# Sums of four rows through TensorE instead of VectorE, thirteen tile places instead of fourteen, and another order

## The chip, the core and the metric

The kernel runs on one core of a Trainium2 chip. Its engines are TensorE (PE, with its weight loads as PEld), VectorE (DVE), ScalarE (ACT), GpSimd (POOL) and SyncE (SP, which here only issues transfers). The metric is the device time of one execution in microseconds (us), the median of several runs; lower is better.

## The reference

The input x is [8, 512, 1024] in float32. Each of the 8 batches is cut into 8 blocks of 64 tokens, and the blocks are summed. The 64 sums go through one matrix (Wk), are normalised, scored against a query vector and turned by a softmax into 8 weights for each batch. The weighted sum of the blocks goes through a second matrix (Wo) and gives one row p of 1024 numbers for each batch, which is added to every token of the batch. Then comes a layer norm, and x itself is added:

```python
block_repr = inputs.reshape(B, n_blocks, block_size, H).sum(axis=2)
keys = jnp.einsum('bnh,kh->bnk', block_repr, Wk)
rms = jnp.sqrt(jnp.mean(keys * keys, axis=-1, keepdims=True) + EPS)
scores = jnp.einsum('bnh,h->bn', keys / rms * rms_weight, q)
attn = jax.nn.softmax(scores, axis=-1)
attended = jnp.einsum('bn,bnh->bh', attn, block_repr)
proj = jnp.einsum('bsh,kh->bsk', broadcast(attended), Wo)
x = inputs + proj
out = (x - mean(x)) / jnp.sqrt(var(x) + EPS) * ln_gamma + ln_beta
return inputs + out
```

## The kernel before, in words

The 4096 tokens are 32 rows of 128 tokens, each a [128, 1024] piece of float32, numbered 0 to 31. Two rows form a tile of 1 MB, and tiles live in places of SBUF (`XSLOTS`, line 20: fourteen). The eight tiles of the two weight matrices (w0 for Wk, w1 for Wo) pass through the same places ahead of the rows. The batches are taken in three groups of 2, 4 and 2 (`GROUPS`, line 19): rows 0 to 7, 8 to 23, 24 to 31; x1.3 is tile 3 of group 1. Rows are finished in units of four or two (`UNITS`, line 21): unit 0 has rows 0 to 3, unit 2 rows 8 to 11, unit 3 rows 12 to 15, unit 7 rows 28 and 29, unit 8 rows 30 and 31.

Each group n goes through these steps, whose names the texts use (n or the row's number k stands behind the letter):

- bs: PE sums a tile's tokens into the block sums in PSUM (line 429); col turns them into columns (DVE, line 439).
- proj n.0: the blocks times Wk (PE, line 473). The softmax steps sm n follow: sq, qk, sdd, mm, v, ln, ex, n1, n2, n3, sc, mx, ex0, rc, wc, small steps that pass between ACT, DVE, POOL and PE (lines 492 to 518). proj n.1: the blocks times Wo; v n w scales the result by the weights (line 529). For group 0 the weights must first be transposed: T0.e and T1.e are the eight transposes by PE of one piece of a matrix, with a copy from PSUM by ACT or DVE.
- p n mm: PE spreads p to all 128 partitions in PSUM (line 545), two copies (cp0, cp1) bring it to SBUF as `pb`, and four small transfers (tb) put its rows into a table `tab` beside gamma and beta.
- S k: DVE adds p to row k in place and sums the result (line 646). Q k: ACT squares the sum less its mean and sums the squares (line 648).
- Unit steps U q: variance (v), its root (std) and inverse root (rs) by POOL, the statistics table (s2, sd2), its transposes by PE (mm, line 721) and their copy to SBUF (lt). Unit 8 takes logarithm and exponential on ACT (ln, ex) instead.
- D k: DVE writes (gamma + std) times row k into a pair of PSUM banks (line 746). R k: PE adds the terms with mean, beta and p, two rows at once (line 732). E k: ACT scales the result by rs back into the row's place (line 761). A store of each finished tile follows on SP.

There are three pairs of PSUM banks and two single ones; a step that needs a pair waits until the last user has read it. Fillers are matmuls of zeros (line 869) between the real ones on PE.

Every step is put down once with the engines that can do it, and the order in which all engines get their steps is written out as one string of step numbers (`ORDER`, line 43; a letter picks the engine, a number behind a colon the bank, f, h and z are fillers). Each engine works through its steps in that order and waits where an operand or a place is not free. Loads are issued by SP in the order of `LOADS` (line 35).

The code already has a kind 'p' of unit (line 633) beside the kind 'c' that all nine units use (`UKIND`, line 26). In kind 'p' the row is not rewritten: its sum is taken from x alone ahead of time (B k), and x + p exists only in PSUM:

```python
for h in range(2):
    nc.tensor.matmul(pair(y)[:, h, :].rearrange("p (q d) -> p q d", d=P), ident, bands(x_row(k))[:, :, h, :],
                     start=True, stop=False, skip_group_check=True)
spread_p(G, y, False)
```

Of the kernel before, what the change touches and what calls it, by code (L numbers as in the profile page):

```python
# [903 lines left out]
```

## Time and profile before

| | us |
|---|---|
| median of 3 runs | 146.02 (145.58 to 146.04) |
| the profiled execution | 144.9 |
| its span | 143.2 |
| PE, DVE, ACT, POOL busy | 112.3, 95.5, 90.9, 58.5 |

The page gives the busy time of each engine over the whole span. Windows give the same for a stretch, the timeline gives single instructions with what ended the idle time before them, and the list of groups gives the mean of one instruction of a form. The mean granted clock of TensorE was 0.932 of full speed.

### The profile page before, as it was taken

What the parts mean: (1) busy time and instruction counts of PE and PEld (TensorE: products, weight loads), DVE (VectorE), ACT (ScalarE), POOL (GpSimd) and SP (SyncE); (2) the same over time, 40 slices, a digit from 0 to 9 for tenths busy, and PEclk for the clock granted to TensorE, in tenths of its full rate; (3) what the DMA queues carried; (4) which work ended last, traced back from release to release, by engine and by line L of the source; (5) the groups of instructions that cost most, each with busy time, mean ns of one, the idle gap of its engine ahead of it and who ended that gap; (6) DMA issues with size and microseconds to landing.
All of it is one profiled execution on the core that took longest, in us unless ns stands there. A gap on an engine that the chain in (4) does not pass through costs nothing.

```text
span 143.2 us, 2871 instructions
## 1 busy us (share of the span) xinstructions
PE 112.3 (78%) x1093; PEld 58.9 (41%) x1101; DVE 95.5 (67%) x161; ACT 90.9 (64%) x140; POOL 58.5 (41%) x107
## 2 busy tenths in 40 slices
PE   7869853989999685999693989989798498496820
PEld 2539652947985222544340335443252132122300
DVE  3040312311315996928879999999999999997930
ACT  3022520024931898255689989899989989989630
POOL 6888800000000066652000895566506928809100
PEclk9995999599999999999999599999999869999965
DMA  4999999999999999605499870724770850775993
...
DMA packets 7526, 42.76 MB, mean 299 GB/s; under 512 B 808, under 2 KB 808, under 8 KB 3672
## 3 DMA queue, kind: packets, MB, share of 16 engines
...
## 4 chain that ended last, share of the span: by engine, by line
DMA 33%; PE 24%; DVE 17%; ACT 11%; issue 6%; POOL 3%; SPq 2%; DVEq 0%; ACTq 0%
PE b L473 11%; DVE t L746 9%; DMA gam<-in_L_cond_ln_gamma_dram 8%; DMA x<-in_L_cond_Wo_dram 8%; DMA x<-in_L_cond_Wk_dram 6%; DMA x<-in_x_dram 5%; PE t L732 5%; PE t L407 4%; ACT x L761 4%; DVE x L646 4%; ACT square L648 3%; DMA tab<-in_L_cond_ln_gamma_dram 3%; DMA pb<-in_cond_dram 3%; ACT woT L241 2%; PE b L429 1%
## 5 line engine op out<-in xcount | busy, mean ns | idle before, releaser
L746 DVE SCALAR_TENSOR_TENSOR t<-gam,ustd,x 128x1024 f32<-128x1024 f32 x31 | 39.1, 1291 | 3.7 <-ACT x L761 2.5
L648 ACT ACTIVATE square<-x,tot 128x1024 bf16<-128x1024 f32 x32 | 36.7, 1147 | 3.3 <-DVE x L646 2.1
L646 DVE SCALAR_TENSOR_TENSOR x<-x,pb 128x1024 f32<-128x1024 f32 x32 | 37.6, 1223 | 0.1
L761 ACT ACTIVATE x<-t,urs 128x1024 f32<-128x1024 f32 x31 | 33.2, 1107 | 5.5 <-PE t L732 2.4
L700 POOL TENSOR_SCALAR stat<-tot 128x8 f32<-128x8 f32 (+1 forms) x8 | 7.5, 934 | 53.1 <-DVE x L646 53.0
L732 PE MATMUL t<-tab,lt 32*128 32x512 f32 x124 | 24.9, 667 | 4.8 <-DVE lt L243 2.2
L407 PE MATMUL t<-ident,x 128*128 128x128 f32 x120 | 17.9, 316 | 5.3 <-DMA x<-in_L_cond_Wk_dram 3.0
L869 PE MATMUL b<-zeros 128*128 128x512 bf16 (+1 forms) x57 | 18.2, 439 | 2.1 <-DVE zeros L294 1.0
L407 PEld LDWEIGHTS t<-ident,x 128*128 128x128 f32 x120 | 16.9, 202 | 6.6 <-issue 4.7
L869 PEld LDWEIGHTS <-zeros 128*128 128x128 bf16 x87 | 8.7, 108 | 17.2 <-issue 12.8
L695 POOL TENSOR_TENSOR ustd<-uv,halfs 128x4 f32<-128x4 f32 (+1 forms) x8 | 13.3, 1660 | 5.5 <-DVE uv L692 4.1
L732 PEld LDWEIGHTS t<-tab,lt 32*128 32x128 f32 x124 | 7.5, 191 | 16.9 <-DVE t L746 5.7
L241 ACT COPY wkT<-t 128x1024 f32<-128x1024 f32 x5 | 5.1, 1013 | 14.1 <-PE t L407 14.1
L715 POOL TENSOR_TENSOR urs<-uv,halfs 128x4 f32<-128x4 f32 (+1 forms) x8 | 13.2, 1650 | 0.0
L243 DVE COPY wkT<-t 128x1024 f32<-128x1024 f32 x3 | 3.7, 1225 | 12.1 <-PE t L407 12.1
L429 PE MATMUL b<-x,blk 128*32 128x256 f32 x128 | 8.4, 384 | 4.2 <-DMA x<-in_x_dram 3.7
L473 PE MATMUL b<-wkT,blkT 128*32 128x256 f32 x192 | 11.0, 380 | 0.6 <-DVE blkT L439 0.6
L241 ACT COPY woT<-t 128x1024 f32<-128x1024 f32 x6 | 5.8, 1014 | 7.8 <-PE t L407 7.8
L429 PE MATMUL t<-x,blk 128*32 128x256 f32 x128 | 7.9, 382 | 3.1 <-DMA x<-in_x_dram 3.1
L473 PEld LDWEIGHTS b<-wkT,blkT 128*32 128x32 f32 x192 | 5.9, 110 | 5.8 <-issue 1.2
L473 PE MATMUL b<-woT,blkT 128*32 128x256 f32 x128 | 7.9, 382 | 0.0
L869 PE MATMUL t<-zeros 128*128 128x512 bf16 x22 | 6.4, 380 | 1.1 <-ACT lt L241 0.6
...
## 6 DMA issues: line engine op xcount, KB each, us to landing
...
```

Of the source, the lines that this page charges most:

```text
L241: nc.scalar.copy(dst, src)
L407: nc.tensor.transpose(half(part, c // 4)[:, bass.ts(c % 4, P)], tile_of(name)[:, e % RT, c::HC], ident)
L429: nc.tensor.matmul(bank(f"bs{n}")[32 * j : 32 * j + 32, :QU], blk[G["g"]], tile_of(name)[:, r, bass.ts(j, QU)], start=(t == 0 and r == 0), ...
L473: nc.tensor.matmul(bank(name)[32 * j : 32 * j + 32, :QU], b[:, c, :], w[:, c, j], start=(c == 0), stop=(c == HC - 1),)
L646: add(f"S{k}", [(DVE, 1.15)], lambda e: nc.vector.scalar_tensor_tensor(x_row(k), x_row(k), 1.0, pb[n], ALU.mult, ALU.add, accum_out=total) ...
L648: add(f"Q{k}", [(ACT, 1.28)], lambda e: nc.scalar.activation(square, x_row(k), AF.Square, bias=total, scale=-float(H), accum_out=ssq), rea ...
L695: add(f"{T} std", [(POOL, 0.5 + 0.16 * U)], lambda e: nc.gpsimd.tensor_tensor(std, v, halfs[:, :1].to_broadcast([P, U]), ALU.pow), reads=[ ...
L715: add(f"{T} rs", [(POOL, 0.5 + 0.16 * U)], lambda e: nc.gpsimd.tensor_tensor(rs, v, halfs[:, 1:].to_broadcast([P, U]), ALU.pow), reads=[V, ...
L732: nc.tensor.matmul(half(f"row{k}", h), lts[q % NST][lo : lo + 32, r // RT, :], tab_of(k)[0][lo : lo + 32, :], start=False, stop=True, skip ...
L746: add(f"D{k}", [(DVE, 1.21)], lambda e: nc.vector.scalar_tensor_tensor(flat(pair(name)), gam, std, x_row(k), ALU.add, ALU.mult), reads=["g ...
L761: add(f"E{k}", [(ACT, 1.13)], lambda e: nc.scalar.activation(x_row(k), flat(pair(name)), AF.Identity, scale=rs), reads=[RS], writes=[xk(k) ...
L869: nc.tensor.matmul(bank_at(i)[:, :n], zeros, zeros[:, 0:1].to_broadcast([P, n]), start=start, stop=True, skip_group_check=True)
```

## The change

Unit 3 (rows 12 to 15) becomes of kind 'p'. Its four S and the Q's that read SBUF go. In their place come B12 to B15, the sums of x alone, each on ACT or DVE; Bp1.0, the sum of p; U3 to, which adds the two sums on POOL; Y12 to Y15 on PE, two matmuls of the row by the identity and the four matmuls of p into the same pair of banks; Q12 to Q15, which square from PSUM; U3 sn, one more small step on POOL; tx1, which multiplies the table by gamma (DVE, 128x512) for this unit's R; and gx, a table of gamma that it needs (one memset and four small loads). `XSLOTS` goes from 14 to 13, some small tiles share storage (`kw` and `diag` now lie in `vw0`), and other kinds and switches that are not used come in. The core of the diff:

```diff
-XSLOTS = 14
+XSLOTS = 13
-UKIND = 'ccccccccc'
-TABS = ((0, 'y'), (1, 'y'), (2, 'y'))
-FORMS = ('y',)
+UKIND = 'cccpccccc'
+TABS = ((0, 'y'), (1, 'x'), (1, 'y'), (2, 'y'))
+FORMS = ('x', 'y')
...
-    kw = alloc("kw", [P, QU], BF16) if junk is None else junk[:, :QU]
+    kw = vw[0]
...
-        elif kind_of(k) == "p":
-            add(f"B{k}", [(ACT, 1.28)], lambda e: nc.scalar.activation(square, x_row(k), AF.Identity, accum_out=usx[u][:, r : r + 1]),
+        elif kind_of(k) in "pa":
+            sx = usx[u][:, r : r + 1]
+            add(f"B{k}", [(ACT, 1.34), (DVE, 1.2)], lambda e: nc.scalar.activation(
+                square, x_row(k), AF.Identity, accum_out=sx) if e == ACT else nc.vector.tensor_reduce(sx, x_row(k), AX.X, ALU.add),
                 reads=[xk(k)], writes=[f"usx{u}.{r}"])
...
-        if mine & set("bp"):
-            add(f"Bp{n}.0", [(ACT, 1.28)], lambda e: nc.scalar.activation(square, pb[n % 2], AF.Identity, accum_out=t[:, 0:1]),
+        if mine & set("bpa"):
+            add(f"Bp{n}.0", [(ACT, 1.34), (DVE, 1.2)], lambda e: nc.scalar.activation(
+                square, pb[n % NPB], AF.Identity, accum_out=t[:, 0:1]) if e == ACT else nc.vector.tensor_reduce(
+                t[:, 0:1], pb[n % NPB], AX.X, ALU.add),
```

The order string is another one. Told by engines, with the steps around the change (S, D and so on of consecutive rows drawn together):

```
DVE before, from the first softmax to S0: qk sdd v n1 n2 n3 sc mx | T1.7 cp0 | rc wc | v0 w | p0 cp0 | S0
DVE after:   qk sdd | T1.6 cp | v | T1.3 cp | n1 n2 n3 sc mx | T1.7 cp1 cp0 | rc wc | B12 B13 | v0 w | B14 | p0 cp1 | S0
DVE before, from S7: S7 | gamma scaled | col1 | D0-D2 | sm1 qk sdd | D3 | v | D4 | n2 n3 sc mx | D5 | U1 lt | rc wc | D6 D7 | S8-S15 | D8 D9 | col2 | D10 | S16-S18 | D11 D12 | sm2 qk | S19 ...
DVE after:   S7 | col1 | U0 lt | D0-D2 | U1 v | sm1 qk sdd v | D3 | n1 n2 n3 sc mx | D4 | rc wc | D5 D6 | p1 cp1 cp0 | S8-S11 | D7 | S16 | tx1 | S17-S19 | D8 D9 | U2 lt | col2 | D10 | S20 | D11 D12 | U3 lt | sm2 qk | S21 ...
ACT after, from E4: E4 E5 | Bp1.0 | Q8 Q15 Q10 Q14 Q9 Q11 | E6 E7 | Q13 Q19 Q12 Q16 | E8 E9 | Q20 | sm2 sq | Q18 | E10 E11 ...
PE before, from R4: R4 | p1 mm | bs2.0 bs2.1 | R6 | bs2.2 | 9 fillers | bs2.3 | U2 mm | R8 | proj2.0 ...
PE after:    R4 | p1 mm | Y15 Y14 | bs2.0 bs2.1 | R6 | Y13 | bs2.2 | Y12 | U2 mm | bs2.3 | R8 | proj2.0 ...
PE, group 0: before T1.7 | proj0.1 | bs1.0 | p0 mm; after T1.7 | bs1.0 | proj0.1 | bs1.1 | p0 mm
SP before: x2.0 | tb0 | x2.1 | st1 st3 | x2.2 | tb1 with st5 | x2.3 | st7 ...
SP after:  x2.0 | tb0 | st1 st3 | x2.1 | st5 | tb1 | x2.2 x2.3 | st7 ...
```

The scaling of gamma goes from DVE to ACT (behind Q5), both copies of p1 from ACT to DVE, the copies lt of units 2, 3, 4 and 7 from ACT to DVE, U1's from DVE to ACT, U7 v from DVE to POOL. In the tail ACT now does U8 ln, E26, U8 ex where it did U8 ln, U8 ex, E26.

## Rows read from the trace of the kernel before

**Rows 1.** The page: busy time, share of the span, instructions of each engine.
```profile
PE 112.3 (78%) x1093; PEld 58.9 (41%) x1101; DVE 95.5 (67%) x161; ACT 90.9 (64%) x140; POOL 58.5 (41%) x107
```

**Rows 2.** Windows: start:end, length, busy of each engine, clock, DMA share, GB/s.
```profile
73.60:128.80 55.20, 45.31 (x339) 18.29 (x334) 54.64 (x84) 51.58 (x80) 30.30 (x28) 0.94 0.56 230
```

**Rows 3.** Groups by form: busy us, mean ns, idle before and its releaser.
```profile
L746 DVE SCALAR_TENSOR_TENSOR t<-gam,ustd,x 128x1024 f32<-128x1024 f32 x31 | 39.1, 1291 | 3.7 <-ACT x L761 2.5 <-ACT u L484 0.8 <-PE t L869 0.3
L646 DVE SCALAR_TENSOR_TENSOR x<-x,pb 128x1024 f32<-128x1024 f32 x32 | 37.6, 1223 | 0.1
L648 ACT ACTIVATE square<-x,tot 128x1024 bf16<-128x1024 f32 x32 | 36.7, 1147 | 3.3 <-DVE x L646 2.1 <-ACT lt L241 0.5 <-ACT square L648 0.3
L761 ACT ACTIVATE x<-t,urs 128x1024 f32<-128x1024 f32 x31 | 33.2, 1107 | 5.5 <-PE t L732 2.4 <-POOL urs L715 1.3 <-issue 1.1
...
L780 DVE TENSOR_SCALAR x<-b,urs 128x512 f32<-128x512 f32 x2 | 1.4, 749 | 0.6 <-PE b L732 0.6
```

**Rows 4.** Timeline of DVE: start us, length us, engine, line, operation.
```profile
75.92 1.22 DVE L646 SCALAR_TENSOR_TENSOR x<-x,pb 128x1024 f32<-128x1024 f32 x1
...
77.07 1.22 DVE L646 SCALAR_TENSOR_TENSOR x<-x,pb 128x1024 f32<-128x1024 f32 x1
...
82.80 2.49 DVE L746 SCALAR_TENSOR_TENSOR t<-gam,ustd,x 128x1024 f32<-128x1024 f32 x2
...
124.75 0.42 DVE L243 COPY lt<-b 128x256 f32<-128x256 f32 x1
125.09 1.22 DVE L646 SCALAR_TENSOR_TENSOR x<-x,pb 128x1024 f32<-128x1024 f32 x1
```

**Rows 5.** Timeline of ACT: two squares in a stream, two scalings.
```profile
76.17 1.15 ACT L648 ACTIVATE square<-x,tot 128x1024 bf16<-128x1024 f32 x1
...
77.45 1.15 ACT L648 ACTIVATE square<-x,tot 128x1024 bf16<-128x1024 f32 x1
...
79.87 2.10 ACT L761 ACTIVATE x<-t,urs 128x1024 f32<-128x1024 f32 x2
```

**Rows 6.** Timeline from the second matrix's transposes to col1, PE and DVE.
```profile
33.60 2.03 PE L407 MATMUL t<-ident,x 128*128 128x128 f32 x16
...
39.30 3.70 PE L459 MATMUL t<-woT,blkT 128*32 128x192 f32 x128
...
45.74 1.23 DVE L646 SCALAR_TENSOR_TENSOR x<-x,pb 128x1024 f32<-128x1024 f32 x1
...
52.36 1.07 PE L429 MATMUL t<-x,blk 128*32 128x256 f32 x16 [0.66 <-DMA x<-in_x_dram]
...
54.88 1.07 PE L429 MATMUL t<-x,blk 128*32 128x256 f32 x16 [1.13 <-DMA x<-in_x_dram]
...
56.14 0.69 DVE L352 TENSOR_SCALAR gam<-gam 128x1024 f32<-128x1024 f32 x1 [1.10 <-DMA gam<-in_L_cond_ln_gamma_dram]
...
56.75 0.44 DVE L439 STREAM_TRANSPOSE blkT<-t 128x256 f32<-128x256 f32 x1
```

**Rows 7.** Timeline of PE from p1's matmuls to proj2.0.
```profile
71.12 1.13 PE L545 MATMUL b<-vw,spread 64*128 64x256 f32 x8
...
78.43 1.07 PE L429 MATMUL b<-x,blk 128*32 128x256 f32 x16 [2.49 <-DMA x<-in_x_dram]
...
83.31 1.07 PE L429 MATMUL b<-x,blk 128*32 128x256 f32 x16
84.32 0.44 PE L721 MATMUL b<-ident,stat 128*128 128x128 f32 x2
...
86.50 3.66 PE L473 MATMUL b<-wkT,blkT 128*32 128x256 f32 x64
```

**Rows 8.** Windows, one late stretch, columns as in rows 2.
```profile
110.00:116.00 6.00, 4.14 (x17) 1.73 (x17) 6.00 (x9) 5.97 (x9) 4.98 (x4) 0.79 0.74 308
```

**Rows 9.** Timeline of SP's queue: the loads of x2.2 and x2.3.
```profile
70.08 0.38 SPq L272 DMA_DIRECT2D x<-in_x_dram  x1
...
76.14 1.25 SPq L272 DMA_DIRECT2D x<-in_x_dram  x1
```

More of the change, by code (lines that the diff above doesn't have):

```diff
@@ L32 @@
 UP = 32768.0
+ADD_ISSUE = 1.3
+BY_PE = ()
+ROOT_POW = ()
+DIVIDE = False
+ADD_MB = 2.0
 SINGLE = (28, 29, 30)
@@ L388, in table @@
                 out=t[32 * q + 2 : 32 * q + 2 + g, :], in_=p[0:P:w, i * HALF : (i + 1) * HALF]),
-                reads=[f"pb{n % 2}.{j}" for j in range(2)], writes=[f"tab{n % NTAB}.{q}"], mb=0.01)
+                reads=[f"pb{n % NPB}.{j}" for j in range(2)], writes=[f"tab{n % NTAB}.{q}"], mb=0.01)
         if (n, "x") in TABS:
@@ L464, in project @@
                     add(f"{name}.{at}.{c0}.{qs}.{cs}", [(PE, 0.012 * cs + 0.108 * qs * cs)], lambda e, go=go: go(),
-                        reads=[f"blkT{n % 2}"] + w_keys(which, range(2 * at, 2 * (at + qs)), halves[0]),
+                        reads=[f"blkT{n % NBT}"] + w_keys(which, range(2 * at, 2 * (at + qs)), halves[0]),
                         claim=("b", name) if at == c0 == 0 else None, use=[] if at == c0 == 0 else [name])
@@ L477, in project @@
             add(f"{name}.{c0}", [(PE, 0.98)], lambda e, go=go: go(),
-                reads=[f"blkT{n % 2}"] + w_keys(which),
+                reads=[f"blkT{n % NBT}"] + w_keys(which),
                 claim=None if c0 else ("b", name), use=[name] if c0 else [])
@@ L514, in softmax @@
             cs, cs, AF.Exp, bias=mx, scale=-1.0, accum_out=es), reads=["mx"], writes=["cs", "es"])
[L515 removed]
+        if not DIVIDE:
+            add(f"{T} rc", [(DVE, 0.18)], lambda e: nc.vector.reciprocal(es, es), writes=["es"])
         add(f"{T} wc", [(DVE, 0.22)], lambda e: nc.vector.scalar_tensor_tensor(
[L517 to L518 removed]
+            kw[:, :NBLK], cs, es, diag8, ALU.divide if DIVIDE else ALU.mult, ALU.mult, accum_out=wcol),
+            reads=["cs", "es", "diag8"], writes=["wcol", "vw0"])
     def bands(row):
@@ L644, in moments, with go @@
                 reads=[S], writes=[Q], use=y, release=[y, y])
+        elif kind in "ad":
+            if place[k][1] % RT == 0:
+                tile_ = x_name(k)
+                add(f"A{k}", [(POOL, ADD_ISSUE)], lambda e: nc.gpsimd.dma_start(
+                    out=tile_of(tile_), in_=pb[n].unsqueeze(1).to_broadcast([P, RT, H]), accum_op=ALU.add),
+                    reads=p_keys, writes=[xk(k), xk(k + 1)], mb=ADD_MB)
+            if kind == "a":
+                add(f"Q{k}", [(ACT, 1.34)], lambda e: nc.scalar.activation(
+                    square, x_row(k), AF.Square, bias=total, scale=-float(H), accum_out=ssq), reads=[xk(k), S], writes=[Q])
+            else:
+                b = ubn[:, k % 2]
+                add(f"B{k}", [(DVE, 1.3)], lambda e: both_halves(b, x_row(k)), reads=[xk(k)], writes=[f"ubn{k % 2}"])
+                add(f"C{k}", [(DVE, 0.2)], lambda e: nc.vector.bn_aggr(out=umv[u][:, r, :], in_=b),
+                    reads=[f"ubn{k % 2}"], writes=[f"umv{u}.{r}"])
+        elif k in BY_PE:
+            y = f"y{k}"
+            def go():
+                for h in range(2):
+                    nc.tensor.matmul(pair(y)[:, h, :].rearrange("p (q d) -> p q d", d=P), ident, bands(x_row(k))[:, :, h, :],
+                                     start=True, stop=False, skip_group_check=True)
+                spread_p(G, y, False)
+            add(f"Y{k}", [(PE, 2.75)], lambda e: go(), reads=["ident", xk(k), "vw0", f"spread{g}"], claim=("t", y))
+            add(f"V{k}", [(ACT, 1.3)], lambda e: nc.scalar.activation(
+                bands(x_row(k)).rearrange("p q i d -> p i q d"), pair(y).rearrange("p i (q d) -> p i q d", d=P),
+                AF.Identity, accum_out=total), writes=[xk(k), S], use=y, release=[y, y])
+            add(f"Q{k}", [(ACT, 1.28)], lambda e: nc.scalar.activation(
+                square, x_row(k), AF.Square, bias=total, scale=-float(H), accum_out=ssq), reads=[xk(k), S], writes=[Q])
         else:
@@ L685, in unit @@
                 a, umv[u][:, :U, 1], UP * UP, pmv[n][:, 2:3], ALU.mult, ALU.add),
-                reads=[f"umv{u}.{r}" for r in range(U)] + [f"pmv{n}.2"], writes=[f"ua{u}"])
+                reads=[f"umv{u}.{r}" for r in range(U)] + [f"pmv{n}.2"], writes=[A])
             add(f"{T} vc", [(E, c)], lambda e: engine[e].tensor_scalar(v, ssq, 2.0 / H * UP * UP, 0.0, ALU.mult, ALU.add),
                 reads=Q4, writes=[V])
-            add(f"{T} v", [(E, c)], lambda e: engine[e].tensor_tensor(v, v, a, ALU.add), reads=[f"ua{u}"], writes=[V])
+            add(f"{T} v", [(E, c)], lambda e: engine[e].tensor_tensor(v, v, a, ALU.add), reads=[A], writes=[V])
+        elif UKIND[q] == "d":
+            add(f"{T} v", [(E, c), (DVE, 0.18)] if slow else [(E, c)], lambda e: engine[e].tensor_scalar(
+                v, umv[u][:, :U, 1], UP * UP, EPS * UP * UP, ALU.mult, ALU.add),
+                reads=[f"umv{u}.{r}" for r in range(U)], writes=[V])
         else:
```

73 lines of the change are left out of this document (40 added, 33 removed), and 43 rows, old and new, of the table ORDER.

## The prediction, made before the changed kernel was run

> **What bounds the kernel now.** I read the page's busy shares first: PE 78%, DVE 67%, ACT 64% of the span [rows 1]. No engine is full on average, so the next view is the windows. From the first summing step after the second projection (S8, 73.6 us) to the last variance steps (128.8 us), DVE is busy 54.64 of 55.20 us, ACT 51.58, PE 45.31, POOL 30.30 [rows 2]. That stretch, 39% of the span, is DVE's. The list of groups tells what fills it: S (1.223 us) and D (1.291 us) on DVE, Q (1.147) and E (1.107) on ACT [rows 3]. The timeline gives the price in a stream, which is less, since one instruction starts before the last has ended: S after S 1.15 us (77.07 less 75.92), two D's 2.49, so 1.2 each, a table copy "lt" 0.34 (125.09 less 124.75) [rows 4]; on ACT Q after Q 1.28 (77.45 less 76.17), two E's 2.10, so about 1.0 each [rows 5]. Ahead of S8 the kernel waits for loads until gamma's row is there at 56.14 [rows 6], and then for the chain softmax, second projection, p.
>
> **The change, part by part.** All times are of the profiled execution (span 143.2, itself 144.9 us; the median of the timed runs is 146.02, 1.1 above it, so I work out a difference and put it on the median).
>
> *Up to S8.* Before proj0.1 the new DVE order puts two copies of transposed weights (T1.6, T1.3) between the steps of the first softmax. A copy of 1024 columns holds DVE no longer than an S does, so that chain ends some 1.3 us later; T1.7's transposes, which need its bank, slip by 0.7 of it. After them PE now does bs1.0 ahead of proj0.1 (1.07, as bs1.7). So proj0.1 starts at about 39.3 + 0.7 + 1.1 = 41.1 and with its 3.70 us ends at 44.8 [rows 6]. The new row sums B12 to B14 (DVE) and B15 (ACT) read x only. No row shows such a reduction; DVE's scaling of gamma, 1024 columns with one operand, took 0.69 [rows 6], an S with two and a sum 1.223 [rows 3]; I take 1.2, S being the one that also sums. By the loads' spacing (bs1.6 and bs1.7 released at 52.36 and 54.88, 2.5 us a tile [rows 6]) rows 12 and 13 land at 42.4, so B12 and B13 end at 44.7, hidden under the wait for proj0.1; if that cover were gone they would cost 2.4. B14 and B15 lie beside bs1.1 and p0's matmuls. S0 comes at 47.7 instead of 45.74: 2.0 late, and S7 ends at 56.9. But before, DVE sat idle 1.10 us there and then scaled gamma for 0.69, and only then came col1 at 56.75 [rows 6]. Scaling has gone to ACT, so col1 starts at 56.9: the two microseconds are swallowed but for 0.15. Two of the four fillers between col1 and proj1.0 have moved inside proj1.0: it ends within 0.2 us of before. ACT, late with its Q's, scales gamma from 56.9 to 58.0 and D0 starts 0.9 later. The second softmax gains: its variance step no longer stands behind D3, n1 goes from POOL to DVE, and its reciprocal stands behind one product instead of a product and a table copy. The two nearly cancel. p's matmuls come at 71.0 (71.12 [rows 7]); both copies of p are now DVE's, 1.3 us, and S8 starts at 73.4 instead of 73.64: **-0.25**. D7, done before S8 until now, comes after it.
>
> *DVE's list from S8 on.* Four S's go: 4 x 1.145 = **-4.6**. D7: **+1.2**. The product tx1 (128x512, two SBUF operands): no row; half an S is 0.6, a 512-column step reading PSUM 0.75 [rows 3]; taken **+0.65**. Table copies of units 2, 3, 4 and 7 move from ACT: 4 x 0.34 = **+1.35**. U7 v moves to POOL: **-0.1**. With the start that is **-1.75**.
>
> *ACT.* Bp1.0 (1.3) comes in, four table copies (1.4) go. Q of rows 12 to 15 reads PSUM; E, which reads PSUM, takes 1.107 and Q 1.147 [rows 3], so between -0.2 and 0 for four: 0. ACT keeps its 3.6 us of slack [rows 2]. POOL's two new small steps (U3 sn, U3 to) are queued before U2's and done while that unit's squares are still running: 0.
>
> *PE, where the change collects its price.* A Y is two fp32 matmuls of 512 columns over all 128 rows and the four of p. Not shown as such. Nearest rows: proj, 64 records in 3.66 us, is 8 steps of 256 columns (four in one step side by side), 0.457 each, so 512 columns are 0.9; p's four take 1.13 alone, two steps of 0.457 at best; 0.95 taken [rows 7]. Y = 2 x 0.9 + 0.95 = 2.75. From above 3.0 (with 1.13 and a weight load not hidden); from below 2.0, if the first two ran at the rate of the transposes by the same identity (128 columns, 16 in 2.03 us, so 0.5 for 512 [rows 6]). I take 2.75, the form being proj's. Queue after p's matmuls at 72.1: Y15, Y14 to 77.6; bs2.0, bs2.1 to 79.7; R6 (waits D7, which ends at 79.2: Q15 is done at 77.3, so D7 does not wait) to 80.8; Y13 to 83.5; bs2.2 84.6; Y12 87.3; U2's transposes 87.75; bs2.3 88.8. Before, bs2.3 ran at 83.31 and U2's transposes at 84.32 [rows 7]. DVE, having ended D9 at 86.75, now stands at U2 lt until 87.8 and at col2 until 88.85. Behind it wait D10, S20, D11 and so all that is left. Idle: 1.0 + 0.75 = **+1.75**. ACT waits at Q12 too, inside its slack. Then R8 and proj2.0 end at 93.5 against 90.2 [rows 7], but the softmax's steps and p2 are placed later in DVE's order and E12, E13 come just in time: 0.
>
> The Trainium skill would price Y lower: "TensorE: Matmul & The Clock Gate", section "Back-to-back issue gap", gives 518 cycles for 512 columns, an estimate of 0.65 us for a Y, and 8 us less on PE. This trace's fp32 rows stand at four times that, which is what "FP8 and Floating Point Precision", section "TensorE Precision Notes", says of true FP32 (four passes). By the first the stall would not exist (rival one); I go by the rows.
>
> *Fillers on PE.* 61 follow p1's matmuls before, 39 after. Between 110 and 116 us the granted clock was already 0.79 and DVE busy 6.00 of 6.00 [rows 8], so a slower clock late costs 0 to 0.5; taken 0, since DVE ran through it.
>
> *Thirteen places.* x2.1 must now wait for the first store's place, x2.2 and x2.3 for the second and third. Such loads were issued at 70.08 and 76.14 and bs2.2, bs2.3 began at 78.43 and 83.31 [rows 7, 9]: 8.3 and 7.2 us. x2.1 goes out at the same point as x2.2 did, lands near 78.4, is wanted at 78.6. x2.2 goes out at 75.7 after p's table rows, lands at 83 to 84, is wanted at 83.5. x2.3 waits for the third store (out at 73.0, done near 80), lands at 87.3 to 88.4, is wanted at 87.75. All just in time: 0, at worst +2.5.
>
> *Tail.* U8's exponent now stands behind E26, 1.0 later, but D28 and D29 run to about then: **+0.1**.
>
> **Sum.** -1.75 + 1.75 + 0.1 = +0.1: 143.3 span, 146.1 on the timed runs. DVE's saved work is spent waiting for PE.
>
> **Rivals.**
> One, PE keeps up (Y near 2.0 us; or the Y's hide in waits that I count as full). Four times 0.75 less on PE, and both of DVE's waits are gone: -1.75 + 0.1 = -1.65, 144.4. For it: PE sat idle 2.49 us before bs2.2 [rows 7], so it has room. Against: fp32 rows of the same form.
> Two, slower: the loads of the last group come late. Place: bs2.1, bs2.2, bs2.3 in PE's queue, in front of R6, Y13, Y12 and all of proj2.0. Price: what they are late by, one for one, since DVE's wait at U2 lt and col2 grows with it. It decides from a landing of x2.1 after 78.6 or x2.3 after 87.75; with 8.3 us and a store done at 81, x2.3 lands at 89.4: +1.6, 147.7. For it: the wait is on a third store instead of a second; against: the queue at that time holds no more bytes than before.
> Three, the change does not shorten DVE at all because E12 to E15 come late on ACT (margins of 0.1 to 0.5 us in my walk): +0.5 to +1, inside the forecast's range.
>
> **How the numbers follow.** Forecast 0.45, its own range 145.5 to 147.1; rival one 0.29; rival two, with all that adds to it, 0.26. A measurement here tells about 0.3% (0.44 us) from no change. Of the forecast's 0.45, 0.29 lie within that, 0.08 on either side. So faster 0.37, same 0.29, slower 0.34. The range runs from rival one to rival two: 144.4 to 147.9.
>
> **What would show it.** Right: in the windows DVE's S x20 in the stretch from S8; PE without gaps from p1's matmuls to proj2.0, a Y at 2.7 to 2.8; DVE idle 1 to 2.5 us at U2 lt and col2 near 87 to 89; bs2.x not waiting for DMA. Wrong: no DVE idle there (rival one); PE idle in front of a bs2, released by DMA (rival two); S8 off 73.4 by over 0.7, which would make the first part wrong.

## The result, and the profile after

The forecast was no change, 146.1 us. The changed kernel is slower: 147.55 us median (146.66 to 148.91, 20 runs) against 145.25 for the kernel before, a ratio of 1.0151 with an interval of 1.0129 to 1.0173. The profiled execution took 147.99 us with a span of 146.2, that of before 144.9 and 143.2: 3.0 us more span, while the medians lie 2.3 us apart. The ratios, and the third experiment's median, leave out executions in a slower state of the chip (one of these 20, five of the twelve there); the other medians do not.

First the page, against [rows 1]:

```profile
PE 118.6 (81%) x1120; PEld 59.5 (41%) x1126; DVE 100.9 (69%) x167; ACT 89.8 (61%) x136; POOL 57.7 (39%) x108
...
PEclk9999999999999999999999999999999996595955
```

PE carries 6.3 us more. DVE shows 5.4 more in spite of the four S's: the row sums and copies of transposed weights ahead of S0, p1's copies and the table copies have come to it. The last line is the clock in 40 slices: full until 120 us, then one 6 and four 5s among 9s, in the last sixth of the span. Keep that place in mind.

The stretch from S8 to the last variance steps, against [rows 2] (start:end, length, busy of each engine with its count, clock, DMA share, GB/s):

```profile
73.46:128.80 55.34, 50.85 (x368) 20.42 (x368) 52.44 (x79) 49.45 (x75) 33.24 (x32) 0.94 0.62 248
```

DVE has 52.44 us of work in it, not 54.64, but it is no longer full: 2.9 us idle. PE has risen from 45.31 to 50.85. The groups by form, against [rows 3]:

```profile
L799 DVE SCALAR_TENSOR_TENSOR t<-gam,ustd,x 128x1024 f32<-128x1024 f32 x31 | 39.0, 1288 | 3.8 <-ACT x L814 2.5 <-POOL ustd L747 0.9 <-ACT square L661 0.2
...
L693 DVE SCALAR_TENSOR_TENSOR x<-x,pb 128x1024 f32<-128x1024 f32 x28 | 33.0, 1221 | 1.0 <-ACT square L695 0.8
L695 ACT ACTIVATE square<-x,tot 128x1024 bf16<-128x1024 f32 x28 | 32.1, 1146 | 3.2 <-DVE x L693 2.8
...
L661 ACT ACTIVATE square<-t,tot 128x1024 bf16<-128x1024 f32 x4 | 4.5, 1114 | 1.6 <-POOL tot L708 1.0 <-PE t L560 0.5
L617 DVE TENSOR_REDUCE usx<-x 128x1 f32<-128x1024 f32 x3 | 3.6, 1212 | 2.1 <-DMA x<-in_x_dram 2.1
```

L799 is D, L693 S, L695 Q from SBUF, L661 Q from PSUM, L617 the new row sums B. Four S's are gone (x28), a row sum costs 1.212 us (the forecast took 1.2), a square from PSUM 1.114 against 1.146. Where DVE stands idle in the middle the timeline of DVE shows (start, length, engine, line, operation, and in brackets the idle time before it and its releaser):

```profile
82.08 1.23 DVE L693 SCALAR_TENSOR_TENSOR x<-x,pb 128x1024 f32<-128x1024 f32 x1 [0.75 <-ACT square L695]
...
86.53 2.58 DVE L799 SCALAR_TENSOR_TENSOR t<-gam,ustd,x 128x1024 f32<-128x1024 f32 x2 [0.92 <-POOL ustd L747]
89.03 0.41 DVE L253 COPY lt<-b 128x256 f32<-128x256 f32 x1
89.53 0.45 DVE L449 STREAM_TRANSPOSE blkT<-b 128x256 f32<-128x256 f32 x1
```

These are S17, D8 with D9, U2 lt and col2. DVE waits 0.75 us at S17 (for Q9, whose sum uses the same place) and 0.92 at D8 (for U2's root on POOL), not at U2 lt and col2. PE in the same stretch:

```profile
72.17 1.98 PE L657 MATMUL t<-x,ident 128*128 128x512 f32 x4 [0.15 <-ACT x L814]
74.08 1.14 PE L560 MATMUL t<-vw,spread 64*128 64x256 f32 x8
75.15 1.98 PE L657 MATMUL t<-x,ident 128*128 128x512 f32 x4
...
84.04 1.07 PE L439 MATMUL b<-x,blk 128*32 128x256 f32 x16
...
88.02 0.44 PE L774 MATMUL b<-ident,stat 128*128 128x128 f32 x2
88.39 1.07 PE L439 MATMUL b<-x,blk 128*32 128x256 f32 x16
```

Behind 72.17 there is not one bracket: PE runs without a gap, a Y every 2.98 us (75.15 less 72.17), and bs2.2 (84.04) and bs2.3 (88.39) wait for no load. S24, before and after:

```profile
109.56 1.22 DVE L646 SCALAR_TENSOR_TENSOR x<-x,pb 128x1024 f32<-128x1024 f32 x1
```

```profile
108.91 1.22 DVE L693 SCALAR_TENSOR_TENSOR x<-x,pb 128x1024 f32<-128x1024 f32 x1
```

It starts 0.65 us earlier than before, but with one D (1.2) less done ahead of it: the hand-over to the last rows is about half a microsecond late. So the middle is nearly as forecast, and most of the loss lies behind it. The tail of the kernel before, POOL (U7's root), PE (R26 and U7 mm) and DVE (D30 and the two halves of E31); the 2.33 us of R26 contain a wait for D27, which its second half needs:

```profile
129.08 0.72 POOL L695 TENSOR_TENSOR ustd<-uv,halfs 128x2 f32<-128x2 f32 x1 [4.14 <-DVE uv L692]
```

```profile
127.77 2.33 PE L732 MATMUL t<-tab,lt 32*128 32x512 f32 x8 [0.21 <-DVE t L746]
130.16 0.33 PE L721 MATMUL b<-ident,stat 128*128 128x128 f32 x1
```

```profile
132.97 1.29 DVE L746 SCALAR_TENSOR_TENSOR t<-gam,ustd,x 128x1024 f32<-128x1024 f32 x1
...
136.33 1.41 DVE L780 TENSOR_SCALAR x<-b,urs 128x512 f32<-128x512 f32 x2 [0.55 <-PE b L732]
```

The tail of the changed kernel: U7's steps on POOL (v, rs, the inverse root; std, the root; sd2), PE (R24, U7 mm, R26), DVE (S31, D27, D29, D30, E31), and the clock in two windows:

```profile
125.89 1.07 POOL L744 TENSOR_SCALAR uv<-ussq 128x2 f32<-128x2 f32 x1
127.05 1.59 POOL L768 TENSOR_TENSOR urs<-uv,halfs 128x2 f32<-128x2 f32 x1
128.61 0.69 POOL L747 TENSOR_TENSOR ustd<-uv,halfs 128x2 f32<-128x2 f32 x1
129.38 1.24 POOL L763 TENSOR_TENSOR stat<-ustd,ind 128x20 f32<-128x20 f32 x1
```

```profile
125.91 2.09 PE L785 MATMUL t<-tab,lt 32*128 32x512 f32 x8
...
130.67 0.33 PE L774 MATMUL b<-ident,stat 128*128 128x128 f32 x1 [1.78 <-POOL stat L763]
...
131.15 1.63 PE L785 MATMUL t<-tab,lt 32*128 32x512 f32 x8
```

```profile
126.83 1.21 DVE L693 SCALAR_TENSOR_TENSOR x<-x,pb 128x1024 f32<-128x1024 f32 x1
...
129.25 1.29 DVE L799 SCALAR_TENSOR_TENSOR t<-gam,ustd,x 128x1024 f32<-128x1024 f32 x1 [1.00 <-ACT x L814]
...
133.94 1.29 DVE L799 SCALAR_TENSOR_TENSOR t<-gam,ustd,x 128x1024 f32<-128x1024 f32 x1 [1.20 <-ACT x L814]
...
136.44 1.29 DVE L799 SCALAR_TENSOR_TENSOR t<-gam,ustd,x 128x1024 f32<-128x1024 f32 x1
...
140.74 1.41 DVE L833 TENSOR_SCALAR x<-b,urs 128x512 f32<-128x512 f32 x2 [1.50 <-PE b L785]
```

```profile
124.00:128.00 4.00, 4.00 (x14) 1.05 (x13) 4.00 (x6) 2.20 (x4) 3.84 (x4) 0.50 0.64 264
...
132.00:136.00 4.00, 3.67 (x16) 1.21 (x13) 2.25 (x4) 2.21 (x3) 1.20 (x1) 0.61 0.73 293
```

Read it backwards. D30 is 3.47 us late (136.44 against 132.97). It stands behind D29, which waits 1.20 us for E26; E26 needs R26; R26 begins at 131.15, because it stands behind U7's transposes on PE, and those wait 1.78 us for POOL. POOL does U7's inverse root ahead of its root, though only the root is on the way to the transposes. Before, R26 ran at 127.77, ahead of U7 mm. U7's own chain is hardly later than before (its root starts at 128.61 instead of 129.08, U7 mm at 130.67 instead of 130.16); it is R26, now behind it, that lost 3.38 us. But the order is not alone in this execution. The clock is at 0.50 from 124 to 128 us, and R24 takes 2.09 us where a clock of 1.00 gives 1.14. E24 comes late behind it, D27 waits 1.00 us for E24 and ends at 130.54, and R26's second half needs D27. The order at full clock is seen in the second experiment and in the new tail on the kernel before.

The span's 3.0 us add up so. S31 [rows 4] starts at 126.83 instead of 125.09 with one D more (1.2) done ahead of it: 0.54 late. From S31 to D30 there are 9.61 us instead of 7.88, again with one D less in it: 9.61 + 1.2 - 7.88 = 2.93 lost. From D30 to E31 0.94 more (4.30 against 3.36, at a clock of 0.5 to 0.6). That is 4.41 at E31; the stores, which now had fallen less behind, end 4.05 instead of 5.46 us after E31's last half has ended, and give back 1.4.

### The profile page after: what moved, and what is told of

The parts are those of the page before. It is cut to its first block, busy times and chain, and to the rows that moved or that the text cites. A ratio compares the mean times of both kernels' runs of the same rounds, so it can differ in the third digit from the quotient of the medians.

```text
span 146.2 us, 2927 instructions
## 1 busy us (share of the span) xinstructions
PE 118.6 (81%) x1120; PEld 59.5 (41%) x1126; DVE 100.9 (69%) x167; ACT 89.8 (61%) x136; POOL 57.7 (39%) x108
## 3 DMA queue, kind: packets, MB, share of 16 engines
q1 hardware_dynamic: 7440, 42.54, 72.4%
## 4 chain that ended last, share of the span: by engine, by line
PE 27%; DMA 27%; DVE 24%; POOL 7%; issue 7%; ACT 4%; POOLq 1%; SPq 0%; DVEq 0%; ACTq 0%
DVE x L693 11%; DMA x<-in_L_cond_Wo_dram 9%; DMA x<-in_x_dram 8%; DVE t L799 7%; PE b L483 7%; DMA x<-in_L_cond_Wk_dram 6%; PE t L657 5%; PE t L785 5%; DMA tab<-in_L_cond_ln_gamma_dram 3%; PE t L560 3%; PE b L439 3%; POOL urs L768 2%; ACT x L814 2%; POOL ustd L747 2%; DMA pb<-n_L_cond_rms_weight_dram 2%
## 5 line engine op out<-in xcount | busy, mean ns | idle before, releaser
L799 DVE SCALAR_TENSOR_TENSOR t<-gam,ustd,x 128x1024 f32<-128x1024 f32 x31 | 39.0, 1288 | 3.8 <-ACT x L814 2.5
L695 ACT ACTIVATE square<-x,tot 128x1024 bf16<-128x1024 f32 x28 | 32.1, 1146 | 3.2 <-DVE x L693 2.8
L693 DVE SCALAR_TENSOR_TENSOR x<-x,pb 128x1024 f32<-128x1024 f32 x28 | 33.0, 1221 | 1.0 <-ACT square L695 0.8
L785 PE MATMUL t<-tab,lt 32*128 32x512 f32 x108 | 22.0, 717 | 3.0 <-DVE t L799 2.2
L922 PE MATMUL b<-zeros 128*128 128x512 bf16 x44 | 15.7, 472 | 4.2 <-DVE zeros L304 2.7
L417 PE MATMUL t<-ident,x 128*128 128x128 f32 x120 | 15.2, 279 | 4.1 <-DMA x<-in_L_cond_Wk_dram 2.5
L417 PEld LDWEIGHTS t<-ident,x 128*128 128x128 f32 x120 | 14.0, 192 | 5.7 <-issue 3.4
L922 PEld LDWEIGHTS <-zeros 128*128 128x128 bf16 x64 | 6.4, 112 | 17.7 <-issue 12.7
L747 POOL TENSOR_TENSOR ustd<-uv,halfs 128x4 f32<-128x4 f32 (+1 forms) x8 | 9.6, 1204 | 4.9 <-DVE uv L744 3.6
L785 PEld LDWEIGHTS t<-tab,lt 32*128 32x128 f32 x108 | 6.0, 193 | 12.1 <-DVE t L799 5.1
L657 PE MATMUL t<-x,ident 128*128 128x512 f32 x16 | 7.9, 618 | 0.2 <-ACT x L814 0.2
```

The source lines that it names most:

```text
L417: nc.tensor.transpose(half(part, c // 4)[:, bass.ts(c % 4, P)], tile_of(name)[:, e % RT, c::HC], ident)
L693: add(f"S{k}", [(DVE, 1.15)], lambda e: nc.vector.scalar_tensor_tensor(x_row(k), x_row(k), 1.0, pb[n], ALU.mult, ALU.add, accum_out=total) ...
L695: add(f"Q{k}", [(ACT, 1.28)], lambda e: nc.scalar.activation(square, x_row(k), AF.Square, bias=total, scale=-float(H), accum_out=ssq), rea ...
L747: add(f"{T} std", [(POOL, 0.5 + 0.16 * U)], lambda e: nc.gpsimd.tensor_tensor(std, v, halfs[:, :1].to_broadcast([P, U]), ALU.pow), reads=[ ...
L785: nc.tensor.matmul(half(f"row{k}", h), lts[q % NST][lo : lo + 32, r // RT, :], tab_of(k)[0][lo : lo + 32, :], start=False, stop=True, skip ...
L799: add(f"D{k}", [(DVE, 1.21)], lambda e: nc.vector.scalar_tensor_tensor(flat(pair(name)), gam, std, x_row(k), ALU.add, ALU.mult), reads=["g ...
```

## The experiments

Theories: ORDER, the loss is in the order of the tail; CLOCK, it is in the granted clock, which the forecast costed at nothing; SUMS, the sums through PE cost more than they save. Each ratio is to the kernel before on the same chip, with its 95% interval. "Loss behind S31" is the time from S31 to D30, with the extra D, against the 7.88 us of the kernel before, in the profiled execution.

**The tail's two late steps (ORDER).**

```diff
-POOL: U7 v | U7 rs | U7 std | U7 sd2
+POOL: U7 v | U7 std | U7 sd2 | U7 rs
-ACT: U8 ln | E26 | U8 ex
+ACT: U8 ln | U8 ex | E26
```

> The changed kernel with two steps of the tail put elsewhere: on POOL unit 7's root and table step ahead of its inverse root, on ACT U8 ex right behind U8 ln and ahead of E26. In the changed kernel the last rows lose about 3.5 us between S31 (126.83) and D30 (136.44, before 132.97). Theory ORDER (the new order of the tail makes U7's transposes and U8's chain late): U7's transposes leave PE by 129.2 instead of 130.67, D30 starts about 1.5 us earlier against S31, ratio to the kernel before 1.004 to 1.008 instead of 1.015. Theory CLOCK (TensorE at its lower clock from 121 us on makes R24, R26, R28 and R31 late): at most 0.5 us, ratio 1.011 to 1.015, the windows behind 121 us still show 0.5 to 0.7.

Measured 146.72 us, 1.0066 [1.0033, 1.01]: more than half of the loss is gone with two steps moved. Loss behind S31: 1.2 us instead of 2.9.

**The clock alone (CLOCK).**

```diff
-PE: 6 fillers | R20 | 6 fillers | R22 | U6 mm ... 3 fillers | U7 mm ... 1 filler | R30
+PE: 10 fillers | R20 | 10 fillers | R22 | 4 fillers | U6 mm ... 8 fillers | U7 mm ... 4 fillers | R30
```

> The changed kernel with 20 fillers more on PE from R20 on (four more ahead of R20 and R22 each, four ahead of U6's transposes, five ahead of U7's, three ahead of R30), nothing else moved. Theory CLOCK: the granted clock stays at or near full behind 121 us, R24 takes 1.1 instead of 2.1 us and R31 half of its time, 1.5 to 2.5 us come back, ratio to the kernel before 0.998 to 1.005. Theory ORDER: the clock may rise but D28 and D30 stay late because they wait for U7's transposes and U8's chain; under 0.7 us come back, ratio 1.010 to 1.015.

Measured 148.11 us, 1.0183 [1.0134, 1.0232], though the clock was 1.00 from 108 to 136 us. CLOCK as the whole cause is refuted. With PE at full speed, D27 is done at 129.31, and U7 mm and R26 behind it still wait for U7's root:

```profile
128.02 1.29 DVE L798 SCALAR_TENSOR_TENSOR t<-gam,ustd,x 128x1024 f32<-128x1024 f32 x1
```

```profile
130.21 0.33 PE L773 MATMUL b<-ident,stat 128*128 128x128 f32 x1 [1.61 <-POOL stat L762]
...
130.69 1.14 PE L784 MATMUL t<-tab,lt 32*128 32x512 f32 x8
```

What the clock itself is worth this does not tell, for the four fillers ahead of R30 also held up the second half of D31 by 0.45 us.

**Both.** The two edits above together.

> Both edits together. Theory CLOCK: as the fillers alone (0.998 to 1.005). Theory ORDER: as the tail's order alone (1.004 to 1.008). If both have a share: their sum, 0.990 to 1.000, which is what my sum for the stretch from S8 on would leave (no change against the kernel before).

Measured 145.82 us, 1.0035 [1.001, 1.0059]: lower than the two steps alone (1.0066), though the intervals overlap, and short of the sum of two shares (0.990 to 1.000).

**Unit 3 back to the old kind (SUMS).**

```diff
-UKIND = 'cccpccccc'
+UKIND = 'ccccccccc'
```

S12 to S15 come back to DVE, B, Bp1.0, tx1, U3 to, U3 sn and the Y's go, 8 fillers stand ahead of U2 mm, and the Q's of rows 9 to 15 stand in the order of their rows; the rest of the order stays but for one small step of U3.

> The changed order and thirteen places, but unit 3 back to the old kind: S12 to S15 on DVE, no Y, B, tx1, U3 to, gx; eight fillers where Y12 stood. It tells the sums through PE from the rest. Theory SUMS COST (the Y's on PE and the waits behind them are what made the kernel slower): ratio to the kernel before 0.99 to 1.005. Theory SUMS PAY (they take 4.6 us from DVE, bring 2 us of waits, and the loss is in the tail): slower than the changed kernel, 1.02 to 1.03, S24 starts 1.5 to 2.5 us later than its 108.9.

Measured 149.16 us, 1.0261 [1.0224, 1.0298], S24 at 110.55 instead of 108.91. SUMS is refuted: in an order written for them the sums through PE are worth 1.1%. Against the order of the kernel before they gain nothing that can be measured, as the last experiment shows.

**U8's exponent alone**, the second line of the first diff:

> The changed kernel with one step moved: U8 ex stands ahead of E26 on ACT again. Two edits together (this one and U7's root ahead of its inverse root on POOL) took 0.85% of the time. If the late exponent is what counts (the step that the prediction priced at 0.1 us), this one alone gives most of it: about 146.7 us, U8 n1 on POOL a microsecond earlier and D30 with it. If U7's chain on POOL is what counts, E26 still comes late behind R26 and D29 still waits for it: 147.3 to 147.8, no measurable gain.

Measured 147.14 us, 1.0104 [1.0038, 1.017], between the two theories and too wide to part them. In the profiled executions D30 follows D29 after 1.88 us here and in the first experiment, after 2.50 in the changed kernel and in the next one: the exponent behind E26 costs 0.62 us up to D30.

**U7's root alone**, the first line of that diff:

> The changed kernel with the other step moved: on POOL U7's root (std) and statistics (sd2) come ahead of its inverse root (rs), as for every other unit. If U7's chain on POOL counts: U7 mm about 1.2 us earlier (129.5 instead of 130.67), R26, E26 and D29 as much, 146.2 to 146.8 us. If the exponent counts: 147.2 to 147.6 us.

Measured 146.74 us, 1.0065 [1.0031, 1.0099]: as good as both steps. U7 mm comes at 129.68 instead of 130.67. DVE's D29 and D30 here:

```profile
132.63 1.29 DVE L798 SCALAR_TENSOR_TENSOR t<-gam,ustd,x 128x1024 f32<-128x1024 f32 x1 [0.75 <-ACT x L813]
...
135.13 1.29 DVE L798 SCALAR_TENSOR_TENSOR t<-gam,ustd,x 128x1024 f32<-128x1024 f32 x1
```

D30 comes 1.3 us earlier, but D29 still waits 0.75 for E26: R26 still stands behind U7 mm. The loss behind S31 is 1.5 us.

**The old tail whole.** From row 24 on every engine has the order of the kernel before:

```diff
-PE: ... R24 | 3 fillers | U7 mm | 1 filler | R26 ...
+PE: ... R24 | 5 fillers | R26 | U7 mm | 4 fillers | R28 ...
-POOL: U7 v | U7 rs | U7 std | U7 sd2 | U8 n1
+POOL: U7 std | U7 sd2 | U8 n1 | U7 rs    (U7 v on DVE)
```

> The changed kernel up to row 23, and from there on every engine in the order of the kernel before (its fillers too, and the three pairs of banks relabelled to fit; U7 v on DVE, R26 ahead of U7 mm). If the whole loss lies in the new order of the tail, only the half microsecond remains by which S24 is behind: 145.6 to 146.0 us, and D30 at most 0.7 us behind the kernel before. If a part of the loss comes from elsewhere (rows 8 to 19, the stores, the clock after the sparser fillers of the middle), it stays at 146.5 us or more.

Measured 146.55 us, 1.0081 [1.0036, 1.0126]: not the 145.6 to 146.0 of ORDER alone, although the profiled execution looks just as ORDER said:

```profile
133.46 1.29 DVE L798 SCALAR_TENSOR_TENSOR t<-gam,ustd,x 128x1024 f32<-128x1024 f32 x1
...
136.83 1.41 DVE L832 TENSOR_SCALAR x<-b,urs 128x512 f32<-128x512 f32 x2 [0.55 <-PE b L784]
```

D30 is 0.49 and E31 0.50 us behind the kernel before, the loss behind S31 is gone. The span is 1.1 us longer than before; the other 0.6 pass behind E31, where only stores are left. And this execution (145.98) was one of its shortest; its timed runs go up to 147.9. Something that differs from one execution to the next takes the rest.

**The new tail on the kernel before.** The reverse edit, on the kernel before:

> The kernel before, with fourteen places and no sums through PE, and from row 24 on every engine in the order of the changed kernel (banks relabelled to fit, U7 v on POOL with the inverse root ahead of the root, R26 behind U7 mm, U8 ex behind E26, the new fillers). If the order of the tail costs what the two kernels with the changed middle say (1.0151 against 1.0081 with the old tail): about 1 us more than the kernel before, 146.6 to 147.2 us, D30 about 3 us later than in the kernel before (132.97). If the tail's order hurts only because the middle hands over late: within 0.4 us of the kernel before.

Measured 149.99 us, 1.0307 [1.0258, 1.0356], three times what was expected. It is not a clean measure: where the two orders are joined DVE waits 1.20 us for U5's root and 0.57 for a scaling. But the tail shows the same picture, with fourteen places and no sum through PE:

```profile
132.35 0.34 PE L721 MATMUL b<-ident,stat 128*128 128x128 f32 x1 [2.69 <-POOL stat L710]
```

U7 mm waits 2.69 us for POOL, and the loss behind S31 is 8.64 + 1.2 - 7.88 = 2.0 us, at a clock of 1.00 from 128 to 136 us: of the order, not of the clock.

**The middle: Q9 early.** On top of the old tail:

```diff
-ACT: Q8 | Q15 | Q10 | Q14 | Q9 | Q11
+ACT: Q8 | Q9 | Q15 | Q10 | Q14 | Q11
```

> As the one with the old order from row 24 on, and Q9 on ACT moved from behind Q14 to right behind Q8, into the microsecond in which ACT waits there for the sum of U3 to. Theory: DVE's two waits in the middle (0.75 us at S17, for the place that unit 2's sum leaves, and 0.92 us at D8, for unit 2's root) hang on a late Q9; they go or halve, S24 comes 0.8 to 1.5 us earlier, and the kernel comes to 144.2 to 145.0 us, level with the kernel before or faster. Rival: DVE's waits hang on PE's queue after all, as the prediction had it; then D9 comes earlier and DVE waits as much at U2 lt and col2: no gain over the other.

Measured 146.61 us, 1.0074 [1.003, 1.0118], the same as without it: the rival. DVE's U2 lt and col2 here:

```profile
88.69 0.42 DVE L252 COPY lt<-b 128x256 f32<-128x256 f32 x1 [1.09 <-PE b L773]
89.72 0.45 DVE L448 STREAM_TRANSPOSE blkT<-b 128x256 f32<-128x256 f32 x1 [0.61 <-PE b L438]
```

S17 and D8 wait no more, and DVE now waits 1.09 and 0.61 us just where the forecast had put 1.0 and 0.75. The two waits stood in front of PE's and hid it; S24 comes at 108.90 instead of 108.86.

**The middle: work put into PE's wait.** On top of Q9 early:

```diff
-PE: bs2.2 | Y12 | U2 mm | bs2.3
+PE: bs2.2 | U2 mm | Y12 | bs2.3
-DVE: U2 lt | col2 | D10 | S20 ... S21        ACT: Q20 ... Q21
+DVE: U2 lt | S21 | col2 | D10 ... S20        ACT: Q21 ... Q20
```

> As the kernel with the old order from row 24 on and Q9 early. There DVE's two waits of 0.75 and 0.92 us were gone, but it waited 1.09 us at U2 lt and 0.61 us at col2 instead, for PE, which ran without a gap from p1's matmuls to proj2.0: the wait that the prediction had sized. Here U2's transposes go ahead of Y12 on PE, and S21, which needs nothing of PE, stands between U2 lt and col2 on DVE (S20 and Q20 take its and Q21's place). Theory: PE's queue is the bound in the middle, and work put into the wait fills it: no wait at U2 lt, under 0.6 us at col2, D10 at about 88.9 us instead of 90.09, S24 at 107.8 to 108.4 instead of 108.90, 145.5 to 146.2 us. Rival: the second group's p comes from PE through the softmax and is as late as before; then DVE only waits later, S24 stays within 0.2 us of 108.90 and the time at 146.6.

Measured 146.47 us, 1.0049 [1.0007, 1.0091]; the rival again. DVE had no wait at U2 lt and 0.58 us at col2, and then waited 0.93 us at D11 for E8 and E9, which come after R8 on PE. The profiled execution was 1.3 us late from U0's table copy on:

```profile
58.72 0.42 DVE L252 COPY lt<-t 128x256 f32<-128x256 f32 x1 [1.36 <-PE t L773]
```

```profile
57.00:58.00 1.00, 1.00 (x3) 0.38 (x2) 0.36 (x1) 1.00 (x2) 0.66 (x2) 0.50 0.36 143
```

Its neighbour had this copy at 57.20 and a clock of 1.00 in the same window. With the shift at S8 taken off (74.88 less 73.56), S24 stands at 108.82. That is where a later theory came from: the clock falls in some executions while PE waits for the loads of bs1.5 to bs1.7. The same execution shows a second dip, and what it costs in the old tail (a window, and D27):

```profile
124.00:128.00 4.00, 3.61 (x11) 1.54 (x15) 4.00 (x6) 3.59 (x6) 2.67 (x3) 0.50 0.79 328
```

```profile
130.49 1.29 DVE L798 SCALAR_TENSOR_TENSOR t<-gam,ustd,x 128x1024 f32<-128x1024 f32 x1 [0.99 <-ACT x L813]
```

R24 takes 2.09 us here, and D27 waits for E24 behind it. In its neighbour the clock is 1.00 there, R24 takes 1.14 us, and D27 does not wait.

**The same without Q9 early.**

> The same edit of PE's and DVE's order without the early Q9. Then DVE still waits 0.75 us at S17 and 0.92 us at D8, and comes to U2 lt and col2 when PE has nearly caught up (0.40 us of wait in the kernel with the old tail): the edit can give 0.4 us at most. Theory of two covering waits: this one stays at 146.3 to 146.7 us, as Q9 alone did, and only both edits together gain. If it gains as much as both together, Q9's place was never of weight.

Measured 147.81 us, 1.0174 [1.013, 1.0218], slower than forecast. Without the early Q9, U2's root is late, and U2 mm, now ahead of Y12, holds up Y12, bs2.3 and proj2.0 behind it:

```profile
87.04 0.44 PE L773 MATMUL b<-ident,stat 128*128 128x128 f32 x2 [1.78 <-POOL stat L762]
```

**Early fillers**, on top of Q9 early and S21:

```diff
-PE: bs1.5 | 3 fillers | bs1.6 | 1 filler | bs1.7
+PE: 3 fillers | bs1.5 | 6 fillers | bs1.6 | 5 fillers | bs1.7
```

> The kernel with the old tail, Q9 early and S21 in front of col2 (1.0049 of before), with ten more fillers on PE in the waits for the loads ahead of bs1.5, bs1.6 and bs1.7. In the profiled execution of that kernel the granted clock was 0.50 from 56 to 58 us and U0's transposes came 1.3 us late, while in its neighbour's it was 1.00 there. Theory: that dip comes in some executions, since PE does little but wait for loads there, and the fillers keep it away: the slowest fast runs (147.6 us) go, median 145.6 to 146.1. Rival: the dips come and go whatever PE does, or the fillers delay bs1.7: 146.3 to 146.8.

Measured 145.55 us (145.09 to 146.49), 1.0011 [0.9982, 1.004], within what the theory said, though the interval touches that of the kernel without them (1.0049 [1.0007, 1.0091]).

**Late fillers as well:** 3 more ahead of R20 and of R22, 4 ahead of U6 mm.

> As the one with more early fillers, and ten more late ones (ahead of R20, R22 and U6 mm, where PE waits for DVE and POOL). If the granted clock of the tail is worth anything when the order of the tail is the old one: 0.2 to 0.5 us less than without them, 145.3 to 145.8. If not: the same within 0.3 us.

Measured 145.14 us (145.00 to 145.62), 0.9983 [0.9963, 1.0003]: level with the kernel before or a trifle faster, and with the least spread so far. From 1.0049 without these fillers to 0.9983 with both: early and late fillers together are worth 0.7% in the mended order.

**The control:** the early fillers on the kernel before.

> The kernel before with the same ten early fillers and nothing else, as the control. If early dips are a trait of the changed order alone: no change within 0.3%. If the kernel before has them too in some executions: 0.2 to 0.5 us faster, and the changed order has gained nothing on it by fillers.

Measured 146.26 us, 1.0051 [1.0028, 1.0074], slower, which neither side expected. The profiled span is 1.3 us longer. From 112 to 120 us its clock was 0.57, before 0.79; S24, S31 and E31 are each half a microsecond late, and the other 0.8 us pass behind E31 (6.26 us instead of 5.46), while stores run. Late fillers on the kernel before were not tried.

**Fillers alone in the changed order:** the early ones, and twelve late ones (4 more ahead of R20 and R22, 4 ahead of U6 mm).

> The changed kernel in its own order, with 22 more fillers on PE (ten ahead of bs1.5 to bs1.7, twelve ahead of R20, R22 and U6 mm; none ahead of R30, where fillers had delayed the last rows). If order and clock each cost their half and add up: the fillers take back about 0.6%, 1.007 to 1.011 of before, 146.5 to 147.1 us, and U7 mm and E26 still come as late as without them. If the clock were the whole cause: 145.5. If fillers help only an order that waits for nothing else: 147.3 to 147.8.

Measured 147.96 us, 1.0139 [1.009, 1.0188], six runs: no gain that can be told.

**Fillers and U7's root.** As the last, with the first line of the first diff.

> The same fillers, and U7's root and statistics ahead of its inverse root on POOL: the smallest mend of both causes, the rest of the order as changed. If the two causes add up (0.85% for POOL's order, about 0.6% for the clock): 1.000 to 1.004 of before, 145.4 to 146.1 us. If more of the tail's order counts (R26 behind U7 mm, U8 ex behind E26): 1.004 to 1.008.

Measured 146.97 us, 1.0075 [1.0037, 1.0113]: no gain over the root alone (1.0065). PE shows why; U7 mm and R26:

```profile
129.48 0.48 PE L773 MATMUL b<-ident,stat 128*128 128x128 f32 x1 [1.92 <-POOL stat L762]
...
130.32 2.09 PE L784 MATMUL t<-tab,lt 32*128 32x512 f32 x8
```

PE waits 1.92 us for U7's root, the clock is 0.57 between 128 and 136 us, and the instruction behind the wait, R26, takes 2.09 us instead of 1.14. That the wait took the clock away is a reading, and not a rule that the runs show: behind the same wait of 1.92 us R26 took 1.31 us with U7's root alone and 1.63 with both steps, and behind 2.69 us, in the new tail on the kernel before, 1.14. In the second experiment more fillers stood ahead of U7 mm and R26 took 1.14 us, but it began at 130.69, as POOL had it: there a full clock could not bring it forward.

**Fillers and the old tail**, without Q9 early and without S21:

> The best one so far (old tail, more fillers; 0.9983 of before) without the early Q9 and without S21 in front of col2. If these two edits of the middle are worth what DVE's waits there said (1.7 us): 146.5 us or more. If PE's queue holds the middle whatever stands in front of it: 145.1 to 145.5 us, the same as with them.

Measured 145.35 us (145.16 to 145.67), 0.9999 [0.9975, 1.0022]. The windows, from row 24 on, of this kernel and then of the changed one:

```profile
108.00:128.00 20.00, 17.33 (x77) 5.96 (x75) 19.85 (x28) 18.07 (x25) 10.52 (x10) 1.00 0.57 233
128.00:143.00 15.00, 7.63 (x32) 2.66 (x32) 8.70 (x16) 7.80 (x11) 3.74 (x4) 0.93 0.73 295
```

```profile
108.00:128.00 20.00, 15.98 (x62) 5.11 (x60) 19.89 (x27) 16.88 (x24) 13.02 (x12) 0.84 0.61 250
128.00:143.00 15.00, 10.04 (x35) 3.31 (x36) 9.27 (x18) 8.90 (x11) 3.74 (x4) 0.73 0.58 234
```

Full clock to 128 us, 7.63 us of PE time behind it instead of 10.04. The profiled executions of the old tail with and without these fillers don't show the gain on DVE, though (E31 at 136.72 and 136.83); the one without was among the shortest of its kernel. So the two edits of the middle gain nothing that can be measured (0.9999 against 0.9983, intervals overlapping), and four kernels sum it up:

| | fillers as changed | more fillers |
|---|---|---|
| tail as changed | 1.0151 | 1.0139 |
| old tail | 1.0081 | 0.9999 |

Old tail and more fillers together return all of the 1.5%; the old tail alone returns half, the fillers alone nothing that can be told. That the first half is the order's, the reverse edit shows too. That the fillers' half comes through the clock is in part argued: the execution with S21 early shows what a dip costs in this tail, and the runs with more fillers lie closer together (145.16 to 145.67 against 145.94 to 147.9).

## Why the prediction was wrong

**The step that failed** is the one headed Tail, "+0.1". It looked at one exponent on ACT. Measured, the tail cost 2.93 us up to D30 and 0.94 behind it, clock and order together; 2.0 at full clock, with the new tail on the kernel before. The walk stopped at S31 and priced the steps that change engine, not the queues that they move past: "U7 v moves to POOL: -0.1" was a credit on DVE. The list of the new order, too, had named only ACT's line of the tail. Two more had changed: on PE R26 stands behind U7 mm, and on POOL the inverse root (1.59) stands in front of U7's root. Neither was priced. U7's root comes no later than before all the same, since v is ready sooner; with the inverse root out of its way U7 mm came 1.0 us earlier still (129.68). So what costs is that R26, E26, D29 and D30 now stand behind a chain that before had R26 in front of it: R26 is 3.38 us late where U7 mm is 0.51 late. No run moved R26 alone; its share is read from the traces, and the old tail whole, which has it ahead again, shows the loss gone. U8's exponent, which the prediction did see, cost 0.62 us up to D30 instead of 0.1; in the timed runs it is the smaller of the two steps as far as they can tell (1.0104 against 1.0065).

**Fillers on PE, "taken 0".** Wrong, and in a way that hid itself: with the order as changed more of them are worth nothing that can be told (1.0151 to 1.0139), with the old tail 0.8% (1.0081 to 0.9999). The reason given, that DVE was full in a window with a clock of 0.79 [rows 8], held for that window and not for the last rows, where PE is on the path.

**The middle, "-1.75 + 1.75".** Near in its sum: with the old tail and more fillers the kernel is at 0.9999, the no change that was forecast. A part of that is luck: the hand-over is still late there, and the granted clock is higher than in the kernel before (0.97 to 0.991 against 0.917 to 0.97). Point by point:
- S8 at 73.46, said 73.4. Two errors of the walk met there: proj0.1 began at 39.60, not 41.1, and ended at 43.28. B12 and B13 had their load at 42.54, nearly as said (42.4), but with proj0.1 done so early they were no longer hidden, and v0 w came at 44.81 all the same.
- DVE's list: B 1.212 (said 1.2), tx1 0.685 (0.65). Right.
- A Y: 2.98 us, said 2.75, inside its bounds of 2.0 and 3.0. Its two identity matmuls take 1.91 in the stream (said 1.8) and p's four 1.07 (said 0.95). By their own length the two took 1.98, so 0.99 for 512 columns. "FP8 and Floating Point Precision" of the Trainium skill, section "TensorE Precision Notes", has true FP32 as four passes; four times the 518 cycles of "TensorE: Matmul & The Clock Gate", "Back-to-back issue gap", is an estimate of 0.86. The trace agrees with the four passes and stands 0.13 above that estimate.
- DVE's idle time: 0.17 + 0.75 + 0.92 = 1.84, said 1.75, but at other places and of other causes, so the size was luck. The early Q9 showed that PE's queue, the cause it named, stood right behind: 1.09 + 0.61.
- ACT, POOL "0": not quite. U3 to took 2.31 us on POOL and kept ACT waiting 1.03 us in front of Q15. Q9 stands behind it, and by that S17 and D8 wait.
- Hand-over to row 24: half a microsecond late at S31. The old tail with more fillers does not make it good: S31 is 0.39 and E31 0.39 us late there in the profiled executions.

**Thirteen places, 0.** Right: no bs2 waited for a load.

**The rivals.** One (PE keeps up) did not come; Y was slower than forecast. Two named a time, 147.7, close to the 147.55 measured, but its place, a load in front of a bs2, shows no wait; the time was right for a wrong reason and earns the rival nothing. Three was not seen, and the range's upper end was rival two's time. None of them looked behind row 24, where a new order had been written for every engine.

What stays open: what R26's place alone costs; what late fillers would do for the kernel before; why the early ones slow it; and why in the profiled executions with the old tail but few fillers the end came 0.8 us later behind E31 (7.47 us from E31's start to the end of the span, 6.68 with more fillers).
